# Attention's probabilities are scaled on ScalarE instead of VectorE, with one inverse per head and the four turns together

## The chip, the core and the metric

The kernel runs on one core of a Trainium2 chip. The metric is the device time of one launch in microseconds (us); three runs of the kernel before gave 2235.98, 2233.18 and 2235.42, so its median is 2235.42 us. The engines are named here as the profile names them: PE is TensorE (matmuls, with PEld for the weight loads that run beside them), DVE is VectorE, ACT is ScalarE, POOL is GpSimd and SP is SyncE, which only issues transfers. Each engine runs its own list of instructions strictly in order and waits on semaphores for the others.

## The reference

Two layers, each with an attention-like part and a feed-forward part, work on `x` of shape 4 x 512 x 512 (rows b, tokens, channels). Before each part the input is gated by a bidirectional recurrence (two scans over the tokens) over a side input. The change is in the second layer's attention: 16 heads in 4 groups, 128 channels a head, causal softmax:

```python
scores = jnp.einsum('bqgpd,bkgd->bgqpk', q, k) * (SCALE / LAYER_INDEX)
...
scores = jnp.where(causal[None, None, :, None, :], scores, -jnp.inf)
probs = jax.nn.softmax(scores, axis=-1).astype(x.dtype)
ctx = jnp.einsum('bgqpk,bkgd->bqgpd', probs, v).reshape(b, sq, HEADS * KVC)
return jnp.einsum('bse,eh->bsh', ctx, w_dense)
```

Everything is fp32. The softmax of a query row is exp(score - maximum) divided by the sum of these.

## The kernel before

The kernel runs four stages one after the other: the state-space layer, the routed experts (to about 1115 us), the attention (to about 1980 us), and the last feed-forward part. The change touches the attention alone.

The attention loops over 64 heads, numbered here h0 to h63 in the order group, row, head of the group: h0 to h3 are row 0 of group 0, h4 to h7 row 1 of group 0, and so on. For one head, `scores` (L1787) handles four strips of 128 queries. Strip `qi` needs keys up to (qi+1)*128, so the strips are 128x128, 128x256, 128x384 and 128x512. For each strip:

- PE multiplies into the PSUM tile `psc` (L1799). The tile comes from a pool of four that the keys `pk` and values `pv` of the next row also use, in turn. So the psc of the next head, strip by strip, needs the exp of the head before to have read its tile.
- DVE adds the causal mask (L1802) and takes the negated maximum `nmax` (L1804).
- `nudge()` issues a step of the gates for later parts (scans L259, L265 and elementwise work L276 to L333 on DVE; `f`, `eu`, `rec` on ACT), which are worked off beside the attention.
- ACT computes `pr` = exp(psc + nmax) and, in the same instruction, the sum `rsum` (L1809, which the profile shows as L128, the line of a helper; a short ACTIVATION_READ_ACCUMULATOR follows).
- DVE takes the inverse (L1810), multiplies `pr` by it (L1811), and turns it in 32x32 blocks into `turned` (L1815).

After the four strips POOL issues four transfers of `turned` to DRAM (L1823), and later `collect` (L1841) issues the one that brings the head back as `pT`, the transposed probabilities. `settle` runs `context` three heads later: PE multiplies `pctx` = v * pT (L1868), ACT copies it to `cx`, and when a row's four heads are there, `dense` multiplies them with w_dense into `pd` (L1887, four tiles of four products) and DVE adds it to the residual `xr` (L1895).

The last two heads (h62, h63; `turn` is true) keep their probabilities in SBUF, and PE turns them (L1854).

What sets the order: a scheduler builds each engine's list from the program; `with after(engine)` pins an instruction behind the one issued before it on that engine. From h13 to h61 (`even[0]` is true) the order on PE is pinned: psc, a query's products (pq, L1750), a key or value product, pctx, one of the four pd tiles. For h0 to h12 the scheduler places PE's work itself, and there all four pd tiles of a row stand together (13.7 us of PE). In the same stretch each new row b+1 of the residual must first be completed: ACT scales the expert results `rr` (L1537), DVE adds them (L1538), PE turns them into `pcb` (L1543), DVE adds that to `xr` (L1547); then ACT loads another activation table (L115), computes `th` of xr, DVE forms the gated input `h` (L406), ACT loads the exp table again, and PE starts the next row's `pq` (L1727), `pk` (L1699) and `pv` (L1710). `Tables.use` places a table load behind all exps, tanhs and the like issued before it; a plain multiply or copy on ACT is not among these. `pq` and `pcb` share a pool of two PSUM tiles.

```python
def ps_mm(name):
    return ps.tile([P, 512], F32, tag="mm", name=name, bufs=4)
```

Of the kernel before, what the change touches and what calls it, by code (L numbers as in the profile page):

```python
# [10 lines left out]
F32 = mybir.dt.float32  # L11
F32R = mybir.dt.float32r
I32 = mybir.dt.int32
AF = mybir.ActivationFunctionType
ALU = mybir.AluOpType
# [3 lines left out]
P = 128  # L19
B, T, C = 4, 512, 512  # L20
NC = C // P
NT = T // P
# [61 lines left out]
def block_kernel(ctx: ExitStack, tc: tile.TileContext, a: dict, out: bass.AP):  # L84
    nc = tc.nc

    @contextmanager
    def after(*engines):

        with ExitStack() as es:  # L90
            for e in engines:
                last = next(
                    (i for i in reversed(nc.cur_bb.bb.instructions) if i.engine == e.engine), None
                )
                if last is not None:
                    es.enter_context(tc.issue_after(last))
            yield
# [35 lines left out]
    act = Tables()  # L133
# [9 lines left out]
    def ps_mm(name):  # L143
        return ps.tile([P, 512], F32, tag="mm", name=name, bufs=4)
# [247 lines left out]
    def nudge():  # L392
        old = list(unsent)
        next(making, None)
        if old:
            send()
# [506 lines left out]
    with ExitStack() as ph:  # L903
# [5 lines left out]
        sm = ph.enter_context(tc.tile_pool(name="ssm", bufs=1, reuse_waits="tile"))  # L909
# [651 lines left out]
    with tc.tile_pool(name="moe_w2", bufs=1, reuse_waits="tile") as wm:  # L1561
# [33 lines left out]
        n = len(nc.cur_bb.bb.instructions)  # L1595
# [15 lines left out]
    with att as ph:  # L1611
        wdp = ph.enter_context(tc.tile_pool(name="att_wd", bufs=1, **right))
        sm = ph.enter_context(tc.tile_pool(name="att", bufs=2, **right))
# [70 lines left out]
        def in_turn():  # L1684
            return after(*[nc.tensor] * even[0])
# [101 lines left out]
        def scores(u, i, qT):  # L1787

            turn = u.last_row and i >= HPG - 2
            prs = []  # L1790
            if not turn:
                blocks = turned[next(numbers) % 2]
            for qi in range(NT):
                n = (qi + 1) * P
                if qi == 0:
                    collect(1)
                psc = ps_mm("psc")
                with in_turn():
                    nc.tensor.matmul(  # L1799
                        psc[:, :n], lhsT=qT[:, qi * P : n], rhs=u.kT[:, :n], start=True, stop=True  # L1800
                    )
                nc.vector.tensor_tensor(psc[:, qi * P : n], psc[:, qi * P : n], mask, ALU.add)  # L1802
                nmax = sm.tile([P, 1], F32, tag="nmax", name="nmax", bufs=4)
                nc.vector.tensor_reduce(nmax, psc[:, :n], AX.X, ALU.max, negate=True)  # L1804
                with after(nc.vector, nc.scalar):
                    nudge()
                pr = sm.tile([P, n], F32, tag=f"pr{qi}", name="pr")
                rsum = sm.tile([P, 1], F32, tag="rsum", name="rsum", bufs=4)
                act(pr, psc[:, :n], AF.Exp, bias=nmax, accum_out=rsum)  # L1809
                nc.vector.reciprocal(rsum, rsum)  # L1810
                nc.vector.tensor_scalar(pr, pr, rsum, None, ALU.mult)  # L1811
                if turn:
                    prs.append(pr)
                    continue
                nc.vector.transpose(  # L1815
                    blocks[:, :, 3 * qi : 4 * qi + 1, :].rearrange("p c k j -> p k c j"), pr
                )
            if turn:
                return prs
            d = turned_d.pop(0)  # L1820
            turned_d.append(d)
            for r in range(QUAD):
                nc.gpsimd.dma_start(  # L1823
                    out=d[:, :, r].rearrange("c i s -> i c s"),
                    in_=blocks[r * SQ : (r + 1) * SQ].rearrange("i c k j -> i c (k j)"),
                )
            away.append(d)
            return d
# [6 lines left out]
        def collect(rest=0):  # L1835

            while len(away) > rest:
                d = away.pop(0)
                back[id(d)] = pT = new_pT()
                with after(nc.gpsimd):  # L1840
                    nc.gpsimd.dma_start(  # L1841
                        out=pT.rearrange("p r k j -> p (r k j)"),
                        in_=d.rearrange("c i r s -> (c i) (r s)"),
                    )
# [128 lines left out]
        for n, (g, b, i) in enumerate(heads_):  # L1973
# [7 lines left out]
            if g == 2 and i == 0 and b < 3:  # L1981
                to, name = ((ffg_d, "gateT"), (ffu_d, "upT"), (ffd_d, "downT"))[b]
# [16 lines left out]
            if g == 0 and i == 2 and b + 1 < B:  # L1999
# [3 lines left out]
                act.use(act.LOG_EXP)  # L2003
                mix(b + 1, h)
            prs = scores(u, i, qT)
            if g == 0 and i == 1 and b + 1 < B:
                with after(nc.scalar):
# [23 lines left out]
    with ExitStack() as ph:  # L2031
        wf = ph.enter_context(tc.tile_pool(name="ff_w", bufs=1, reuse_waits="tile"))
        sm = ph.enter_context(tc.tile_pool(name="ff", bufs=2, **right))
# [201 lines left out]
```

## Time and profile before

| what | us |
|---|---|
| three runs | 2235.98, 2233.18, 2235.42; median 2235.42 |
| profiled execution, its time | 2229.05 |
| its span, first to last instruction | 2227.1 |
| outside the span (2229.05 - 2227.1) | 1.95 |
| PE busy | 2115.8 (95%) |
| DVE busy | 1584.9 (71%) |
| ACT busy | 952.4 (43%) |
| POOL busy | 500.2 (22%) |

The profiled execution is 6.4 us below the median of the three runs. Busy time is the sum of an engine's instructions; an engine that is idle has waited for something, and the profile names what came last. Two stretches of the attention differ:

| stretch, us from the span's start | PE busy | DVE busy | ACT busy | mean granted PE clock |
|---|---|---|---|---|
| 1115 to 1325 (h0 to h12) | 186.54 of 210 | 171.06 | 95.51 | 0.94 |
| 1325 to 1945 (the rest) | 615.54 of 620 | 468.37 | 218.26 | 0.99 |

### The profile page before, as it was taken

To read this page: it belongs to the slowest core of one execution; us is meant where nothing else is said; L and a number is where in the kernel's file an instruction comes from. 1 tells how busy PE (TensorE), PEld (TensorE's weight loads), DVE (VectorE), ACT (ScalarE), POOL (GpSimd) and SP (SyncE) were. 2 spreads that over 40 slices of the span, in tenths; PEclk is the share of its full clock that TensorE was granted. 3 is DMA by queue.
4 is the path that set the end of the run, shared out by engine and by line. 5 is a ranking of instruction groups with operands and counts; after the bars stand their busy time and mean duration, and the time that the engine had idled before them with its cause. 6 is when DMAs were issued, how large, how long until landed. Compare 5 with 4: busy or idle time off the path is not lost. (4 is left out here: it accounts for less than half of the span.)

```text
span 2227.1 us, 24718 instructions
## 1 busy us (share of the span) xinstructions
PE 2115.8 (95%) x7858; PEld 1283.1 (58%) x7858; DVE 1584.9 (71%) x3207; ACT 952.4 (43%) x1875; POOL 500.2 (22%) x668
## 2 busy tenths in 40 slices
PE   4979999999999999999988999999999999999998
PEld 2545565555665444444444446666666666568887
DVE  8698989999653566576479877788888766654332
ACT  4576676775732234333155433333333322333221
POOL 4023232422222111222233222222122222100000
PEclk9989999999999999999999999999999999999999
DMA  7542251442424458988577676767777565621100
GB/s 256 187 142 77 95 170 67 140 139 67 166 86 133 151 198 288 379 288 296 204 241 267 215 258 201 228 207 231 219 231 229 177 212 150 226 84 38 38 20 20
DMA packets 125512, 390.99 MB, mean 176 GB/s; under 512 B 15360, under 2 KB 36224, under 8 KB 111872
## 3 DMA queue, kind: packets, MB, share of 16 engines
q1 hardware_dynamic: 90560, 249.60, 32.6%
q0 software_dynamic: 32512, 135.55, 19.6%
q10 hardware_dynamic: 2304, 4.20, 0.5%
q8 instruction: 65, 1.06, 0.2%
q14 instruction: 71, 0.58, 0.1%
HBM read 363.07 MB, written 116.39 MB: 215 GB/s over the span
## 5 line engine op out<-in xcount | busy, mean ns | idle before, releaser
L128 ACT ACTIVATE pr<-psc,nmax 128x128 f32<-128x128 f32 (+3 forms) x256 | 134.1, 525 | 361.0 <-DVE nmax L1804 360.7
L1823 POOL DMA_DIRECT2D turned<-turned x248 | 135.7, 554 | 581.9 <-DVE turned L1815 501.5
L1887 PE MATMUL pd<-cx,wd 128*128 128x512 f32 x512 | 228.5, 593 | 0.0
L1799 PE MATMUL psc<-kT,qT 128*128 128x128 f32 (+3 forms) x512 | 158.0, 447 | 14.9 <-ACT pr L128 14.9
L1895 DVE TENSOR_TENSOR xr<-xr,pd 128x512 f32<-128x512 f32 x64 | 43.9, 685 | 175.5 <-PE pd L1887 175.4
L1868 PE MATMUL pctx<-pT,v 128*128 128x512 f32 (+3 forms) x512 | 151.9, 441 | 8.4 <-DMA pT<-turned 8.4
L1057 PE MATMUL pc<-h,wxb 128*128 128x512 f32 x320 | 145.5, 610 | 6.5 <-DVE h L406 4.0
L1887 PEld LDWEIGHTS pd<-cx,wd 128*128 128x128 f32 x512 | 93.8, 191 | 98.8 <-issue 97.4
L1868 PEld LDWEIGHTS pctx<-pT,v 128*128 128x128 f32 x512 | 97.1, 193 | 74.2 <-issue 51.1
L847 PE MATMUL po<-w,yT 128*128 128x512 f32 x296 | 134.1, 593 | 0.2 <-ACT yT L840 0.2
L814 PE MATMUL pg<-w,hT 128*128 128x512 f32 x296 | 134.2, 594 | 0.0
L825 PE MATMUL pn<-w,hT 128*128 128x512 f32 x296 | 133.3, 592 | 0.0
L1799 PEld LDWEIGHTS psc<-kT,qT 128*128 128x128 f32 x512 | 87.4, 193 | 69.7 <-issue 27.4
L1815 DVE STREAM_TRANSPOSE turned<-pr 128x128 f32<-128x128 f32 x248 | 120.4, 497 | 0.3
L1804 DVE TENSOR_REDUCE nmax<-psc 128x1 f32<-128x128 f32 (+3 forms) x256 | 120.1, 479 | 0.4
L1128 PE MATMUL pz<-wzt,h 128*128 128x512 f32 x256 | 116.1, 602 | 0.3 <-ACT st L1229 0.3
L1276 PE MATMUL po<-wot,yT 128*128 128x512 f32 x256 | 115.5, 605 | 0.0
L1057 PEld LDWEIGHTS pc<-h,wxb 128*128 128x128 f32 x320 | 60.9, 195 | 78.8 <-issue 72.8
L1811 DVE TENSOR_SCALAR pr<-pr,rsum 128x128 f32<-128x128 f32 (+3 forms) x256 | 103.8, 410 | 0.8
L1750 PE MATMUL pq<-ht,wq 128*128 128x256 f32 x384 | 98.5, 379 | 0.0
L1171 ACT ACTIVATE lm<-lm,cs 128x128 f32<-128x128 f32 x256 | 81.8, 390 | 22.5 <-DMA lm<-cs 22.5
L825 PEld LDWEIGHTS pn<-w,hT 128*128 128x128 f32 x296 | 54.8, 190 | 61.7 <-issue 61.7
(367 smaller groups left out, 4505.9 us busy)
## 6 DMA issues: line engine op xcount, KB each, us to landing
w<-in_w1x SPq DMA_DIRECT2D x76, 1024.0 KB
turned<-turned POOLq DMA_DIRECT2D x248, 208.0 KB, 4.0
pT<-turned POOLq DMA_DIRECT2D x62, 832.0 KB, 7.6
w<-in_w2x SPq DMA_DIRECT2D x38, 1024.0 KB
wb<-in_b1x SPq DMA_DIRECT2D x38, 512.0 KB
lm<-cs SPq DMA_DIRECT2D x32, 512.0 KB
kt<-in_fT SPq DMA_DIRECT2D x62, 256.0 KB
ek<-ek SPq DMA_DIRECT2D x62, 256.0 KB
```

The source lines that it names most:

```text
L128: nc.scalar.activation(*args, **kw)
L814: nc.tensor.matmul(pg, lhsT=hT[:, k, :], rhs=self.w1[s][0][:, k, :], start=(k == 0), stop=(k == NC - 1))
L825: nc.tensor.matmul(pn, lhsT=hT[:, k, :], rhs=self.w1[s][1][:, k, :], start=(k == 0), stop=(k == NC - 1))
L847: nc.tensor.matmul(po, lhsT=yT[:, j, :], rhs=self.w2[s][:, j, :], start=(j == 0), stop=(j == NI - 1))
L1057: nc.tensor.matmul(pc, lhsT=wxb[:, k, m * P : (m + 1) * P], rhs=h[:, k, :], start=(k == 0), stop=(k == NC - 1),)
L1128: nc.tensor.matmul(pz, lhsT=w.h[:, k, u.tok], rhs=wzt[:, k, hh * 512 : (hh + 1) * 512], start=(k == 0), stop=(k == NC - 1),)
L1799: nc.tensor.matmul(psc[:, :n], lhsT=qT[:, qi * P : n], rhs=u.kT[:, :n], start=True, stop=True)
L1804: nc.vector.tensor_reduce(nmax, psc[:, :n], AX.X, ALU.max, negate=True)
L1815: nc.vector.transpose(blocks[:, :, 3 * qi : 4 * qi + 1, :].rearrange("p c k j -> p k c j"), pr)
L1823: nc.gpsimd.dma_start(out=d[:, :, r].rearrange("c i s -> i c s"), in_=blocks[r * SQ : (r + 1) * SQ].rearrange("i c k j -> i c (k j)"),)
L1868: nc.tensor.matmul(pctx[:, kj * P :].rearrange("p (q r j) -> p q r j", r=QUAD, j=SQ), lhsT=u.v[:, kj, :], rhs=pT[:, :, 4 * kj : 10 + kj : ...
L1887: nc.tensor.matmul(po, lhsT=dense_w[u.g, m][:, i], rhs=u.ctxT[i], start=(i == 0), stop=(i == HPG - 1),)
```

## The change

Heads h0 to h61 are changed; h62 and h63 do what they did. The four sums of a head go into the columns of one 128x4 tile. After all four exps DVE takes one inverse of the 128x4 tile. ACT then multiplies each strip's `pr` by its column, in place, and DVE turns the strip. So per head four 128x1 inverses and four multiplies leave DVE, one 128x4 inverse comes to it, four multiplies come to ACT, and the four turns of a head, which stood each behind its own strip, stand behind the head's last exp. The transfers are the same and in the same order.

```diff
@@ -1788,6 +1788,7 @@
 
             turn = u.last_row and i >= HPG - 2
             prs = []
+            rsum = sm.tile([P, NT], F32, tag="rsum", name="rsum", bufs=2)
             if not turn:
                 blocks = turned[next(numbers) % 2]
             for qi in range(NT):
@@ -1805,18 +1806,20 @@
                 with after(nc.vector, nc.scalar):
                     nudge()
                 pr = sm.tile([P, n], F32, tag=f"pr{qi}", name="pr")
-                rsum = sm.tile([P, 1], F32, tag="rsum", name="rsum", bufs=4)
-                act(pr, psc[:, :n], AF.Exp, bias=nmax, accum_out=rsum)
-                nc.vector.reciprocal(rsum, rsum)
-                nc.vector.tensor_scalar(pr, pr, rsum, None, ALU.mult)
+                rs = rsum[:, qi : qi + 1]
+                act(pr, psc[:, :n], AF.Exp, bias=nmax, accum_out=rs)
+                prs.append(pr)
                 if turn:
-                    prs.append(pr)
-                    continue
+                    nc.vector.reciprocal(rs, rs)
+                    nc.vector.tensor_scalar(pr, pr, rs, None, ALU.mult)
+            if turn:
+                return prs
+            nc.vector.reciprocal(rsum, rsum)
+            for qi, pr in enumerate(prs):
+                nc.scalar.mul(pr, pr, rsum[:, qi : qi + 1])
                 nc.vector.transpose(
                     blocks[:, :, 3 * qi : 4 * qi + 1, :].rearrange("p c k j -> p k c j"), pr
                 )
-            if turn:
-                return prs
             d = turned_d.pop(0)
             turned_d.append(d)
             for r in range(QUAD):
```

## The prediction

> **What bounds the kernel now.** I read the page's engine rows first, then busy time by stretch, what PE's idle time waited for in each stretch, and single transitions on the timeline.
>
> ```profile
> PE 2115.8 (95%) x7858; PEld 1283.1 (58%) x7858; DVE 1584.9 (71%) x3207; ACT 952.4 (43%) x1875; POOL 500.2 (22%) x668
> ```
>
> PE is busy 95% of the span, and the change leaves PE's work as it is. So it can matter only where PE waits. Next the two stretches of the attention (columns: stretch, its length, busy time and count of PE, PEld, DVE, ACT and POOL, granted clock, DMA share, GB/s):
>
> ```profile
> 1115.00:1325.00 210.00, 186.54 (x611) 100.75 (x612) 171.06 (x373) 95.51 (x205) 69.87 (x99) 0.94 0.73 244
> 1325.00:1945.00 620.00, 615.54 (x2331) 398.14 (x2330) 468.37 (x1320) 218.26 (x560) 146.72 (x264) 0.99 0.68 210
> ```
>
> In the second stretch PE loses 4.5 us in 620, in the first 23.5 in 210. I call the first uneven, the second even. The uneven stretch's waits (what waits, total us, count, longest):
>
> ```profile
> PE psc L1799 <- ACT pr L128: 14.3, 11, 2.8
> PE pctx L1868 <- DMA pT<-turned: 5.5, 2, 5.2
> PE pcb L1543 <- DVE rr L1538: 2.0, 3, 0.7
> PE pq L1727 <- DVE xr L1547: 1.1, 3, 0.5
> ```
>
> The even stretch's:
>
> ```profile
> PE pctx L1868 <- DMA pT<-turned: 2.9, 1, 2.9
> PE ptp L1854 <- DVE pr L1811: 0.9, 1, 0.9
> PE psc L1799 <- ACT pr L128: 0.6, 1, 0.6
> ```
>
> So the even stretch has 4.4 us to give at most, and the change has to pay or cost among h0 to h12. There DVE is full wherever PE stalls (9.8 to 10.0 us of each 10 in 1140-1150, 1170-1180, 1190-1200, 1250-1260 and 1310-1320). The exps that psc waits for wait in turn for DVE's nmax.
>
> **The change, part by part.** The rows it touches, taken over the attention:
>
> ```profile
> L1810 DVE RECIPROCAL rsum<-rsum 128x1 f32<-128x1 f32 x256 | 36.6, 147 | 4.3 <-ACT pr L128 4.2
> L1811 DVE TENSOR_SCALAR pr<-pr,rsum 128x512 f32<-128x512 f32 x64 | 30.2, 472 | 0.3
> L1811 DVE TENSOR_SCALAR pr<-pr,rsum 128x384 f32<-128x384 f32 x64 | 27.6, 431 | 0.3
> L1811 DVE TENSOR_SCALAR pr<-pr,rsum 128x128 f32<-128x128 f32 x64 | 23.6, 369 | 0.1
> L1811 DVE TENSOR_SCALAR pr<-pr,rsum 128x256 f32<-128x256 f32 x64 | 23.5, 367 | 0.1
> L1537 ACT ACTIVATE rr<-rr,g 128x512 f32<-128x512 f32 x12 | 8.3, 720 | 2.6 <-DMA rr<-rows_o 2.5
> ```
>
> *DVE, per head:* four inverses (4 x 0.147 = 0.59) and four multiplies (0.369 + 0.367 + 0.431 + 0.472 = 1.64) go. One inverse of 128x4 comes; its nearest row is the 128x1 at 0.147, I take 0.15 (bounds 0.1 to 0.3, the latter a 128x128 operation's 0.28). Net -2.08 per head, -129 us over 62 heads. Some of the removed time is contention: one 128x128 multiply at 1266.93 runs on to 1271.5 beside POOL's work, where an undisturbed one takes 0.28.
>
> *ACT, per head:* four multiplies with a per-partition scale. The only such row is L1537, 720 ns for 512 columns; for the short ones the exps bound it (367, 469, 579 ns for 128, 256, 384). Sum 0.37 + 0.47 + 0.58 + 0.70 = 2.1 us. Successive instructions overlap by about 0.11 (two L1537 take 1.33), so a group stands for 1.75 us. Over 62 heads 130 us; in the even stretch ACT rises from 35% to about 52%, DVE falls from 76% to about 60%. Below 1.6 or above 2.3 us a head no row reaches.
>
> The Trainium skill ("ScalarE: Activation LUTs", "Rules for kernel authors") speaks against this: simple arithmetic such as multiplication belongs on VectorE, which is said to be faster per element. The rows here agree with the direction: 472 against 720 ns for 128x512. The same page ("What ACT_TABLE_LOAD costs") gives an activation with a per-partition pointer operand about 280 ns plus 0.833 ns a column; as an estimate that makes 2.19 us a head in place of 2.1, or 136 us over the kernel in place of 130. Neither decides, as ACT is half empty; what decides is what stands behind the four multiplies.
>
> *The even stretch.* The four multiplies wait for one inverse, which waits for the last exp; behind them on ACT stand kT or vT copies, the cx copy, and the next head's first exp. I followed the heads at 1506 and 1527. At 1527 the last exp could end at about 1533.8, as nmax no longer stands behind the four inverses and multiplies; multiplies to 1535.65; the kT copy waits for PE's pk at 1535.9, as before. The tightest reader is pd, which needs the fresh cx as its fourth product:
>
> ```profile
> 1537.95 3.60 PE L1887 MATMUL pd<-cx,wd 128*128 128x512 f32 x8
> 1538.21 0.60 ACT L1879 COPY cx<-pctx 128x512 f32<-128x512 f32 x1
> ```
>
> (first line PE, second ACT). It is read at about 1540.5, with the copy done at 1538.8; delayed by even a whole group of 1.75 us it would still be there. At 1506 cx comes about 2.5 us later (1516.7 for 1514.2), with 12 us before its use. The turns end 0.8 us earlier (1517.1 for 1517.9). So nothing in the even stretch costs PE anything; the pT wait of 2.9 us at 1725 shrinks by about 0.3, as the 128x512 turn ends that much earlier. **-0.3 us.**
>
> *The uneven stretch.* Between rows (in heads h1, h5, h9) the expert results are added on a chain that PE waits for: ACT scales rr, DVE adds (L1538), PE makes pcb, DVE adds xr, ACT th, DVE h, then PE's pq. Today rr follows the last exp (its accumulator is read at 1197.21) at once, and the table load lies behind it, under PE's and DVE's work:
>
> ```profile
> 1197.21 0.21 ACT L128 ACTIVATION_READ_ACCUMULATOR pr<-psc,nmax 128x1 f32 x1
> 1197.30 1.33 ACT L1537 ACTIVATE rr<-rr,g 128x512 f32<-128x512 f32 x2
> 1198.65 1.28 ACT L115 ACT_TABLE_LOAD   x1
> 1201.96 1.15 ACT L128 ACTIVATE th<-xr 128x512 f32<-128x512 f32 x2 [2.03 <-DVE xr L1547]
> ```
>
> In the built instruction lists of the changed kernel the order at all three transitions is: last exp, table load, the four multiplies, then rr. So rr comes 1.28 + 1.75 = **3.0 us** later, counted from the last exp. The last exp itself may come earlier, by what DVE is relieved of. PE's side of it today:
>
> ```profile
> 1197.47 2.08 PE L1799 MATMUL psc<-kT,qT 128*128 128x512 f32 x2 [1.28 <-ACT pr L128]
> 1199.49 1.71 PE L1543 MATMUL pcb<-ident,rr 128*128 128x128 f32 x8
> 1201.39 4.56 PE L1727 MATMUL pq<-h,wq 128*128 128x512 f32 x10 [0.19 <-DVE xr L1547]
> ```
>
> pcb already waits for rr at each transition (2.0 us in three waits above), so a later rr is a later PE.
>
> Followed instruction by instruction through DVE's, ACT's and PE's new orders with today's durations, it gives:
> - Row 0 to 1: the stalls of 1143 to 1152 (2.30 + 2.84 + 1.17) stay, since h0's four turns (1.68) now stand together between h1's nmax. PE is 3.0 late at pcb and 4.4 late at 1172 (three turns more between the adds to xr). Then psc's stalls there (1.02 + 1.19 + 1.31 = 3.5) vanish, because the multiplies of h3 no longer hold up its nmax. Left: **+0.9**.
> - Row 1 to 2: psc's third stall group (0.90 + 1.28) shrinks by 0.5, rr costs 3.0, and a wait of pk for 0.5 moves in with it: **+2.2** at 1210.
> - Row 2: DVE's order puts h7's softmax behind the adds from pd, so xr is 0.9 late for pq; h10's stall group grows from 1.95 (1.71 + 0.24) to 2.65: **+1.6**.
> - Row 2 to 3: rr costs 3.0; pcb's and pq's waits there (0.69 + 0.54) and the 4.57 us multiply at 1267 are gone, and only **+0.2** is left by pk.
>
> The wait of 5.2 us for pT at 1314 absorbs none of this: the transfer is issued behind h12's four turns, which come later with everything else. Sum at 1325: 0.9 + 2.2 + 1.6 + 0.2 = **4.9 us**.
>
> *The end.* h61's multiplies hold up h62's first exp by 1.5 us, which psc does not need yet: 0. After new stalls PE runs slower for a while (granted clock 0.81 in 1140-1150, where a 384-column psc pair took 1.65 us, not 0.91): **+0.5**.
>
> Sum 4.9 - 0.3 + 0.5 = +5.1: the profiled execution goes from 2229.05 to 2234.2. That execution is 6.4 under the median; moved onto the median, 2235.4 + 5.1 = **2240.5 us**.
>
> **The rivals.**
> - *No change that can be measured* (0.2%, 4.5 us, is what a measurement of this kernel can tell from none). DVE's relief returns as much as the transitions cost. For it: psc's waits are behind nmax, nmax behind the inverses and multiplies. Against it: the turns now come four in a row, 1.68 us, in front of nmax. About +1, 2236; it happens if half the 3 us at each transition is caught up (3 x 1.5 = 4.5 less).
> - *Faster: DVE bounds the uneven stretch.* Twelve and a half heads give back 12.5 x 2.08 = 26 us of DVE there. If all of psc's 14.3 and 0.6 and pT's 8.4 went, 23.3, it would be 2212. But the six us before the first transition stay, and rr's 9 us must be paid; with the rest of psc's stalls (8) and pT's (8.4) gone and 9 paid: -7.4, 2228. It decides where the last exp of h1, h5, h9 comes over 3.0 us earlier than now.
> - *Slower by more: nothing is caught up.* Three times 4.4 us = 13, with 0.5 of slow clock each: 2235.4 + 14.7 = 2250.
> - *The even stretch breaks:* if ACT's blocked list delays cx, kT or psc by 1 us in each of 12 rows, +12, 2247. Against it: the slack of 1.7 us that was read above, and PE's order is pinned.
>
> **How the numbers follow.** Slower at about 2240 has 0.38, slower by more (by either of the last two) 0.14; no change 0.33; faster 0.15. The likeliest one's own range is 2240 to 2246. The range for 8 in 10 leaves out the far half of either end: 2229 to 2250. Faster by over 0.2%: 0.15; within: 0.33; slower: 0.52.
>
> **What would show it.** DVE should fall to about 1456 us and ACT rise to about 1083. The even stretch should stay within 1 us of its length. At the three transitions the table load and four multiplies should stand between the last exp and rr, and PE's wait of pcb for rr should grow from 2.0 to some 8 us in all. psc's waits should fall from 14.3 to about 11. I am wrong if those transitions do not grow (then no change or faster), or if kT, cx or qT copies show up as what PE waits for in the even stretch.

## The result and the profile after

The changed kernel took 2245.63 us (median of six runs, 2243.79 to 2248.60), the kernel before 2235.28 beside it. The ratio is 1.0053, its 95% interval 1.0039 to 1.0068: slower by half a per cent, some 10 to 12 us, where 5 were forecast. The time lies in the forecast range and on its side. The size is the forecast's doubled, and it takes two steps of the sum to say why.

The busy time of the engines over the changed kernel's span of 2241.8 us, from the first part of its page:

```profile
PE 2121.6 (95%) x7858; PEld 1288.8 (57%) x7858; DVE 1506.7 (67%) x2773; ACT 1064.6 (47%) x2123; POOL 504.6 (23%) x668
```

The 248 multiplies are on ACT and 434 instructions have left DVE. PE has the same 7858 matmuls but 5.8 us more of busy time: it did the same work more slowly.

To find the place I laid fixed points of both traces side by side. The first `pk` of the attention starts at 1115.10 before and at 1119.58 after; these 4.5 us belong to work that both kernels have in common and are not the change's (over all traces of this study the point lies between 1113.88 and 1122.80). They are also why the two profiles lie 14.7 us apart (2229.05 and 2243.79), more than the medians do. From there to the first `pk` of the even stretch (1331.99 and 1349.23) the busy times are, before and after:

```profile
1115.10:1331.99 216.89, 193.53 (x636) 105.34 (x637) 175.36 (x388) 97.51 (x212) 70.99 (x101) 0.94 0.73 243
```

```profile
1119.58:1349.23 229.65, 198.67 (x636) 108.62 (x637) 148.18 (x287) 122.70 (x268) 71.20 (x100) 0.91 0.70 235
```

The stretch is 12.8 us longer. PE's busy time grew by 5.1 (193.53 to 198.67) at a lower granted clock (0.94 to 0.91), and its idle time by 7.6 (216.89 - 193.53 = 23.4; 229.65 - 198.67 = 31.0). DVE lost 27 us there, as intended, and ended up with more idle time. Behind it nothing is lost; in the changed kernel PE is busy without a break from 1344.48 to 1717.00:

```profile
1344.48:1717.00 372.52, 372.52 (x1436) 243.99 (x1435) 272.32 (x616) 192.31 (x467) 87.91 (x157) 1.00 0.71 220
```

and from 1349.23 to the end it is 2.5 us shorter than before (892.6 for 895.1). That is not less waiting but a faster clock: PE's busy time there is 881.9 for 884.9, and before has two spells of 3.4 us at a granted clock of 0.50 (from 1726.45 and 1934.66) that the changed kernel has not. What PE waited for in the first stretch after the change (total us, times, longest):

```profile
PE pcb L1543 <- DVE rr L1538: 11.8, 5, 3.7
PE psc L1800 <- ACT pr L128: 11.1, 11, 3.1
PE pctx L1871 <- DMA pT<-turned: 5.9, 1, 5.9
PE pk L1699 <- DVEq L1601: 2.4, 1, 2.4
PE pq L1727 <- DVE xr L1547: 1.5, 2, 0.9
PE pk L1699 <- ACT pr L128: 0.4, 1, 0.4
```

The `pk` wait for DVEq ends at the start of the stretch and lies ahead of it. Against the list of before: `pcb` rose from 2.0 to 11.8, `psc` fell from 14.3 to 11.1. Not all of `pcb`'s waits lie at the transitions: of the 2.0, 1.3 stand at 1128.08 and 1129.66, beside h0's first strips, and only 0.69 at a transition, the third; of the 11.8, 2.0 stand beside h0's strips and 2.64, 3.50 and 3.66 at the three transitions. So there the wait rose from 0.7 to 9.8. On ACT's timeline of the changed kernel the transition from the second to the third row shows the price of `pcb`:

```profile
1201.46 0.69 ACT L128 ACTIVATE pr<-psc,nmax 128x512 f32<-128x512 f32 x1
1202.03 0.21 ACT L128 ACTIVATION_READ_ACCUMULATOR pr<-psc,nmax 128x1 f32 x1
1202.26 1.28 ACT L115 ACT_TABLE_LOAD   x1
1203.56 1.92 ACT L1819 ACTIVATE pr<-pr,rsum 128x128 f32<-128x128 f32 x4
1205.38 1.32 ACT L1537 ACTIVATE rr<-rr,g 128x512 f32<-128x512 f32 x2
```

`rr` began 0.09 us after the last exp's accumulator read before (1197.21, 1197.30) and begins 3.35 us after it now (1202.03, 1205.38); at the other two transitions it is 3.32 and 3.33. The cause is a line that the diff does not touch: `combine(b + 1, (2, 3))`, which issues `rr`, stands behind `scores` under `with after(nc.scalar)`. That pins it behind whatever ScalarE was given last. Before that was the exp; now it is the fourth multiply, and the scheduler put the table load ahead of the multiplies too.

### The profile page after: what moved, and what is told of

It reads as the page before. It is cut to its first block, busy times and chain, and to the rows that moved or that the text cites. A ratio compares the mean times of both kernels' runs of the same rounds, so it can differ in the third digit from the quotient of the medians.

```text
span 2241.8 us, 24538 instructions
## 1 busy us (share of the span) xinstructions
PE 2121.6 (95%) x7858; PEld 1288.8 (57%) x7858; DVE 1506.7 (67%) x2773; ACT 1064.6 (47%) x2123; POOL 504.6 (23%) x668
## 4 chain that ended last, share of the span: by engine, by line
PE 43%; DVE 3%; DMA 2%; ACT 2%; issue 0%; SPq 0%; POOL 0%; DVEq 0%; POOLq 0%; ACTq 0%
PE pd L1890 10%; PE pq L1750 6%; PE pctx L1871 6%; PE psc L1800 4%; PE pv L1710 2%; PE pk L1699 2%; PE pfo L2068 2%; PE pfo L2067 2%; PE pfg L2067 2%; PE pfg L2068 2%; PE pfu L2067 2%; PE pfu L2068 2%; PE pq L1727 1%; DMA pT<-turned 1%; DVE turned L1820 1%; DMA rr<-rows_o 1%
## 5 line engine op out<-in xcount | busy, mean ns | idle before, releaser
L1800 PE MATMUL psc<-kT,qT 128*128 128x128 f32 (+3 forms) x512 | 155.1, 440 | 12.6 <-ACT pr L128 12.5
L1819 ACT ACTIVATE pr<-pr,rsum 128x128 f32<-128x128 f32 x248 | 118.9, 550 | 16.2 <-DVE rsum L1817 16.2
```

The source lines that it names most:

```text
L1800: nc.tensor.matmul(psc[:, :n], lhsT=qT[:, qi * P : n], rhs=u.kT[:, :n], start=True, stop=True)
```

## The experiments

Theory 1: the cost is made among h0 to h12, where `rr` stands behind multiplies and table load at three transitions, and PE, once it has waited, runs slower for a while. Rivals: ScalarE is too full in the even stretch; the single inverse and the four turns together are the cost, wherever the multiplies run; ScalarE's multiplies hold up exps anywhere in the first stretch.

Every row below is measured against the kernel before. The stretch is the one between these two `pk`; the waits are PE's in it, those of `psc` for the exp alone (in rr_act_only it waits 1.9 us more for a copy of kT).

| kernel | median us | ratio [95%] | stretch us | PE idle | PE busy | pcb | psc |
|---|---|---|---|---|---|---|---|
| before | 2235.28 | 1 | 216.89 | 23.4 | 193.5 | 2.0 | 14.3 |
| the change | 2245.63 | 1.0053 [1.0039, 1.0068] | 229.65 | 31.0 | 198.7 | 11.8 | 11.1 |
| late_only | 2233.05 | 0.9998 [0.9980, 1.0016] | 218.97 | 21.6 | 197.4 | 2.2 | 13.8 |
| early_only | 2246.15 | 1.0054 [1.0033, 1.0075] | 233.22 | 32.3 | 200.9 | 10.9 | 11.1 |
| rr_first | 2229.64 | 0.9974 [0.9955, 0.9992] | 215.55 | 22.2 | 193.3 | 1.8 | 12.5 |
| rr_first_2 | 2227.28 | 0.9984 [0.9967, 1.0001] | 213.49 | 22.1 | 191.4 | 1.8 | 12.6 |
| rr_act_only | 2230.43 | 0.9994 [0.9980, 1.0008] | 216.10 | 22.3 | 193.8 | 3.3 | 9.4 |
| trans_dve | 2232.79 | 1.0005 [0.9992, 1.0017] | 216.79 | 24.8 | 192.0 | 3.9 | 10.4 |
| dve_mul | 2238.41 | 1.0017 [0.9996, 1.0038] | 225.73 | 31.1 | 194.7 | 8.6 | 12.2 |
| dve_rr_first | 2233.24 | 0.9999 [0.9984, 1.0014] | 218.46 | 23.3 | 195.2 | 3.2 | 10.8 |
| per_strip | 2240.99 | 1.0041 [1.0026, 1.0056] | 220.46 | 25.0 | 195.4 | 7.9 | 11.4 |
| warm | 2238.60 | 1.0017 [1.0000, 1.0035] | 222.42 | 17.2 | 205.2, of it 15.9 idle products | 2.1 | 6.6 |
| double_even | 2254.30 | 1.0102 [1.0079, 1.0124] | 233.20 | 32.9 | 200.3 | 12.9 | 11.1 |

The before that the series of experiments ran beside had medians of 2232.81 to 2233.18, so ratios, not medians, are to be compared across rows. One profile a kernel stands behind the last five columns, and PE busy for the same instructions spreads: before and late_only do the same up to h12, and have 193.5 and 197.4.

### Where: late_only and early_only

With `n0` the number of the head, late_only keeps the form of before where `n0 < 13`, early_only where `n0 >= 13`:

```diff
+            old = n0 < 13
...
-                if turn:
+                if turn or old:
                     nc.vector.reciprocal(rs, rs)
                     nc.vector.tensor_scalar(pr, pr, rs, None, ALU.mult)
...
```

> The change for h13 to h61 alone; h0 to h12 keep the form of before. Theory 1 (the whole cost is made among h0 to h12, where rr waits behind the four multiplies): no change that can be measured, 0.998 to 1.002 of before, and PE's waits for psc, pcb and pT in the first stretch of the attention as before (14.3, 2.0, 5.5 us). Rival (ScalarE's blocked list also delays cx, kT or psc in the even stretch): a ratio of 1.003 or more, with new PE waits after h13.

> The change for h0 to h12 alone; h13 to h61 keep the form of before. Theory 1: all of the cost is here, a ratio of 1.004 to 1.007 as in the changed kernel (about +10 us), and PE's wait of pcb for rr among h1 to h12 about 9 us longer than the 2.0 of before. Rival (the even stretch carries the cost): 1.000 to 1.002.

Both came out as theory 1 had them: 0.9998 for 49 heads in the even stretch, 1.0054 for the 13 heads ahead of it, against 1.0053 for all. The rival of a full ScalarE in the even stretch is out: the multiplies of h13 to h61 cost nothing that can be measured.

### What: rr_first, trans_dve, rr_act_only

rr_first issues `rr` behind the last exp of h1, h5 and h9 (`between` is `combine(b + 1, (2, 3))` there, and empty for the other heads), and the head's inverse, multiplies and turns behind it:

```diff
-            nc.vector.reciprocal(rsum, rsum)
+            with ExitStack() as es:
+                if between:
+                    between()
+                    es.enter_context(after(nc.vector))
+                nc.vector.reciprocal(rsum, rsum)
...
```

> The whole change, but in h1, h5 and h9 the results rr are issued right behind the last exp, and the inverse, the four multiplies and the four turns of that head behind them. Theory 1 (the pin of rr behind the last instruction issued on ScalarE, now the fourth multiply, is the cause): pcb's waits for rr fall from about 12 us back to 2 to 5, PE's granted clock at the transitions recovers, and the time is 2231 to 2238. Rival (the grouped turns, or ScalarE's longer list among h0 to h12, cost on their own): the waits of pcb go, but the time stays above 2241, with other waits in their place.

The waits of `pcb` are gone, the time fell from 2245.6 to 2229.6, a little under the 2231 expected, and with the whole change in place it is under the kernel before. ACT's timeline of rr_first at the same transition:

```profile
1196.28 0.69 ACT L128 ACTIVATE pr<-psc,nmax 128x512 f32<-128x512 f32 x1
1196.85 0.21 ACT L128 ACTIVATION_READ_ACCUMULATOR pr<-psc,nmax 128x1 f32 x1
1196.94 1.34 ACT L1537 ACTIVATE rr<-rr,g 128x512 f32<-128x512 f32 x2
1198.30 1.28 ACT L115 ACT_TABLE_LOAD   x1
```

The load stands behind `rr` again, as it did before the change. PE's waits of rr_first in the stretch:

```profile
PE psc L1800 <- ACT pr L128: 12.5, 11, 3.1
PE pctx L1875 <- DMA pT<-turned: 3.5, 1, 3.5
PE pk L1699 <- DVEq L1601: 2.4, 1, 2.4
PE pq L1727 <- DVE h L406: 2.2, 2, 1.8
PE pq L1727 <- DVE xr L1547: 2.1, 2, 1.7
PE pcb L1543 <- DVE rr L1538: 1.8, 3, 0.8
```

New are 2.2 us for `h` and one more for `xr`, where the head's turns now stand; the transfer of pT is 2 us better. The repetition:

> The kernel of rr_first once more, beside the two others. It is expected at 0.996 to 0.999 of before, 2225 to 2231 us, as it measured 0.9974. If the ratio's interval reaches over 1.000 here, its gain over the kernel before is not settled.

It gave 0.9984, with the interval's end at 1.0001. By what was put on record, the gain over the kernel before is not settled; both series point to about 0.2%.

trans_dve gives h1, h5 and h9 the form of before, by the edit of late_only with `n0 in (1, 5, 9)`:

> The change in all heads but h1, h5 and h9, which keep the form of before (inverse, multiply and turn of each strip on VectorE). Theory 1 (three heads carry the cost): 2229 to 2236, pcb's waits among h1 to h12 2 to 5 us. Rival (the ten other heads of the first stretch cost too): 2239 or more.

2232.79, as theory 1 had it. Three heads of 62 carry the cost. The other ten of the first stretch cost nothing that can be measured.

rr_act_only is rr_first without the pin on VectorE (`es.enter_context(after(nc.vector))`):

> As rr_first, but only ScalarE's order is mended: rr stands right behind the last exp there, while inverse and turns of h1, h5 and h9 are left to the scheduler, which puts the four turns of h4 or h5 ahead of the add of rr between the second and the third row. If ScalarE's order alone decides: as rr_first, 2227 to 2233. If VectorE's order counts as well (turns that wait for the multiplies stand ahead of the add of rr): 2233 to 2241, with a wait of pcb of 2 us or more left at that one transition.

2230.43 lies in the first range, and rr_first_2, which ran beside it, lies within its interval (0.9984 in 0.9980 to 1.0008), so the time does not tell the two apart. The trace shows that VectorE's order does count: a `pcb` wait of 2.15 us is left at 1197, at the one transition where the turns stand ahead of the add of `rr`.

### How much is the grouping: dve_mul, dve_rr_first, per_strip

```diff
-                nc.scalar.mul(pr, pr, rsum[:, qi : qi + 1])
+                nc.vector.tensor_scalar(pr, pr, rsum[:, qi : qi + 1], None, ALU.mult)
```

> One inverse of four sums and the four turns together as in the change, but the four multiplies stay on VectorE. Theory 1: rr follows the last exp at once on ScalarE, and only the 0.3 to 0.6 us by which VectorE's multiplies stand ahead of the add of rr are left at each transition, so +0 to +3 us, 2234 to 2239. Rival (the single inverse and the turns together are the cost, wherever the multiplies run): +8 us or more, 2243 and above, with PE's psc and pT waits longer.

The time, 2238.41, lies in theory 1's range, but the way there was not what I wrote: `pcb` still waits 8.6 us. ScalarE's `rr` is prompt (at 1207.47, 0.10 us behind the last accumulator read at 1207.37), yet the four multiplies, which now come together behind the one inverse, stand ahead of the add of `rr` on DVE, and at the first transition the turns too. Of the 8.6 us, 5.3 lie at the three transitions (1.93, 1.17 and 2.19). PE's waits in dve_mul's stretch:

```profile
PE psc L1800 <- ACT pr L128: 12.2, 10, 4.0
PE pcb L1543 <- DVE rr L1538: 8.6, 5, 2.5
PE pctx L1871 <- DMA pT<-turned: 7.5, 2, 6.4
```

So the chain from `rr` to `pcb` can be blocked on either engine. That the grouping alone costs time is likely and not shown, as its ratio's interval reaches 0.9996. dve_rr_first is this edit on rr_first:

> The kernel of rr_first with the four multiplies on VectorE: rr is issued right behind the last exp in h1, h5 and h9, one inverse of four, four turns together. Theory 1 with a gain from the relief of VectorE: slower than rr_first by 2 to 6 us, 2232 to 2236, since the 26 us of multiplies and inverses are back on the engine that psc waits for. Rival (rr_first gains by the order alone, and where the multiplies run is worth nothing): the same as rr_first within 1.5 us.

0.9999: with `rr` first the grouping on DVE costs nothing that can be measured. It is 6 us above rr_first_2 and 3.6 above rr_first, as a gain from VectorE's relief would have it. But the intervals overlap, so that gain is likely and not shown.

per_strip keeps the multiplies on ScalarE, each with an inverse and a turn of its own:

```diff
+                nc.vector.reciprocal(rs, rs)
...
+                nc.scalar.mul(pr, pr, rs)
+                nc.vector.transpose(
+                    blocks[:, :, 3 * qi : 4 * qi + 1, :].rearrange("p c k j -> p k c j"), pr
+                )
...
-            nc.vector.reciprocal(rsum, rsum)
-            for qi, pr in enumerate(prs):
-                nc.scalar.mul(pr, pr, rsum[:, qi : qi + 1])
-                nc.vector.transpose(
...
```

> Four multiplies on ScalarE, but each strip has its own inverse, multiply and turn behind its exp, as before. Theory 1 (rr waits for what stands between the last exp and it on ScalarE): only one multiply of 0.7 us is left behind the last exp, so pcb's waits are 5 to 7 us and the time 2236 to 2241 in place of 2245.6. Rival (any multiply on ScalarE makes the exps wait for VectorE's inverses in between, strip by strip, which the grouping avoids): above 2246.

2240.99, at the upper end; `pcb` 7.9, a little above the 5 to 7, with 6.6 of it at the three transitions. The ratio's interval overlaps that of the change, so the gain over it is not shown by the time. On ACT's timeline of per_strip one sees what I left out, the table load, which stands ahead of the last multiply here too:

```profile
1197.35 0.19 ACT L128 ACTIVATION_READ_ACCUMULATOR pr<-psc,nmax 128x1 f32 x1
1197.56 1.28 ACT L115 ACT_TABLE_LOAD   x1
1198.86 0.72 ACT L1816 ACTIVATE pr<-pr,rsum 128x512 f32<-128x512 f32 x1
1199.49 1.32 ACT L1537 ACTIVATE rr<-rr,g 128x512 f32<-128x512 f32 x2
```

`rr` starts 2.1 us behind the accumulator read, not 0.7: of the changed kernel's 3.35, about 1.3 is the load and 1.8 the four multiplies. No run moves the load alone; its share is read off the timelines.

### The clock: warm

```diff
                 psc = ps_mm("psc")
+                if qi == NT - 1 and (u.g, i) == (0, 2) and u.b < B - 1:
+                    for _ in range(20):
+                        nc.tensor.matmul(
+                            psc[:, :P], lhsT=ident, rhs=ones, start=True, stop=True
+                        )
```

> The change, with twenty idle products of 128x128 (their result is overwritten) put on TensorE ahead of the last psc of h2, h6 and h10, where TensorE stands still for 2.6 to 3.7 us before pcb. Theory 1b (of the 12.8 us lost in the first stretch of the attention, 5.1 are a lower granted clock after these idle times): the same work of PE there goes back from 193.9 us towards 189, and the time from 2245.6 to 2239 to 2242, though PE has more to do. Rival (the clock does not follow the idle time, or the idle time is needed in any case): 2244 to 2248.

PE did 15.9 us more of work and the kernel became faster than the changed one: 2238.60, a little under the 2239 expected, and the intervals of the two ratios do not overlap. The products stand mostly where PE had waited: its idle time fell by 13.8 us (31.0 to 17.2), so they cost 2.1. The gain is in the other work: without them PE's busy time in the stretch is 205.2 - 15.9 = 189.3, against 198.7. PE's timeline of the changed kernel around the first transition (start, us, work, and in brackets the idle time before it):

```profile
1154.36 2.08 PE L1800 MATMUL psc<-kT,qT 128*128 128x512 f32 x2 [0.26 <-ACT pr L128]
1159.08 1.97 PE L1543 MATMUL pcb<-ident,rr 128*128 128x128 f32 x8 [2.64 <-DVE rr L1538]
1161.65 9.02 PE L1727 MATMUL pq<-h,wq 128*128 128x512 f32 x14 [0.61 <-DVE xr L1547]
```

the same `pq` in before:

```profile
1153.91 6.52 PE L1727 MATMUL pq<-h,wq 128*128 128x512 f32 x14 [0.36 <-DVE xr L1547]
```

and that of warm (40 records are 20 products; the last `psc` moved in between the two halves of `pcb`):

```profile
1157.09 6.31 PE L1801 MATMUL psc<-ones,ident 128*128 128x128 f32 x40 [0.25 <-ACT pr L128]
1163.24 0.60 PE L1543 MATMUL pcb<-ident,rr 128*128 128x128 f32 x4
1163.67 1.02 PE L1805 MATMUL psc<-kT,qT 128*128 128x512 f32 x2
1164.54 0.60 PE L1543 MATMUL pcb<-ident,rr 128*128 128x128 f32 x4
1164.97 5.32 PE L1727 MATMUL pq<-h,wq 128*128 128x512 f32 x12
```

A `psc` pair of 512 columns takes 2.08 us in the changed kernel and 1.02 in warm, the `pq` matmuls 0.64 and 0.44 each, and 0.47 in before. The granted clock of the changed kernel at the three transitions (columns as in the windows above, the clock behind POOL's count):

```profile
1150.14:1167.21 17.07, 11.24 (x19) 5.03 (x20) 14.69 (x29) 8.18 (x16) 4.43 (x7) 0.50 0.70 222
1204.75:1214.99 10.24, 7.20 (x15) 4.07 (x16) 6.64 (x12) 4.30 (x9) 2.19 (x4) 0.50 0.83 254
1273.02:1276.43 3.41, 3.41 (x10) 2.42 (x11) 3.38 (x7) 0.52 (x1) 1.77 (x4) 0.50 0.85 286
```

Over the stretch the clock was at half for 40.8 us in the changed kernel, 23.9 in before and 20.5 in warm. PE's work in this time was 30.0, 18.8 and, without the idle products, 14.6 us. Half of the differences, 5.6 us to before and 7.7 to warm, is what the slower clock should cost; measured are 5.1 and 9.4. So idle time at a transition can be paid twice, once as waiting and once as slower work behind it.

The second price does not go by the wait's length. `pcb` waited 2.64, 3.50 and 3.66 us at the three transitions, and half clock lasted 17.1, 10.2 and 3.4. Nor does it go by the idle time of the stretch: dve_mul's PE was idle as long as the changed kernel's (31.1 us) and had half clock for only 26.9 us and 194.7 us of busy time; late_only was idle for 21.6 and had 33.8 and 197.4.

The Trainium skill ("TensorE: Matmul & The Clock Gate", "What's actually happening") says that the clock is gated to half when TensorE has been idle for a window of about 3.4 us. The half is seen here, and the spells at half in the changed kernel last whole multiples of 3.4 us. That it takes one idle stretch of that length is not what these traces show: no gap ahead of the slow `pq` was as long as 3.4 (3.11, 0.26, 2.64 and 0.61 us, with 1.7 to 2.1 us of work between), and the clock was at half from 1150.14, behind the first 0.8 us of the first of them.

### The slack of the even stretch: double_even

```diff
                 nc.scalar.mul(pr, pr, rsum[:, qi : qi + 1])
+                if even[0]:
+                    nc.scalar.copy(pr, pr)
```

> The change, with a copy of each strip in place on ScalarE behind each of its multiplies, in h13 to h61 (about 1.9 us more per head, 93 us more of ScalarE). Theory 1 (the even stretch has ScalarE to spare, some 1.7 us before cx is late): 0 to +4 us on the changed kernel, 2245 to 2250, no new PE waits but single ones. Rival (it is full, and the change only just fits): +10 us or more, with PE waiting for cx, kT or psc.

2254.30, 8.7 above the changed kernel by medians and 11 by ratios (1.0102 and 1.0053 of before): about the rival's 10, and more than theory 1 allowed. ScalarE's busy time rose by 66.7 us (1064.6 to 1131.3), 1.36 a head, less than the 1.9 I expected. Of the profile, 3.6 us lie in the first stretch, which the edit does not touch (233.20 against 229.65, as in early_only), and 7.2 behind it (899.8 against 892.6). PE's waits of double_even behind that stretch:

```profile
PE pctx L1873 <- DMA pT<-turned: 7.8, 3, 3.1
PE psc L1800 <- ACT pr L128: 2.3, 1, 2.3
PE pd L1892 <- ACT cx L1884: 0.4, 1, 0.4
```

In the changed kernel they are 3.2, 1.4 and none, so they grew by 5.9 of the 7.2. So the even stretch has room for one set of multiplies and not for two, and what comes late first is the transfer of pT behind the turns, hardly the `cx` that I had called the tightest.

## Why the prediction was right in kind and short in size

- **The place and the mechanism held.** "The order at all three transitions is: last exp, table load, the four multiplies, then rr. So rr ... 3.0 us later": the trace has 3.3 (3.35 less 0.09), early_only has the whole cost, and rr_first takes it away. One reading on the way was wrong: "pcb already waits for rr at each transition (2.0 us in three waits above)". Of these three waits two lie beside h0's strips, and only the third transition had one (0.69).
- **The even stretch, "-0.3 us":** right as far as can be told. late_only measured 0.9998, in an interval of 0.18% (4 us) to either side, and the changed kernel's PE had no break up to 1717; 0.3 us itself is below what the runs resolve.
- **psc "from 14.3 to about 11":** 11.1. DVE's relief was worth what the working said, and it did make good the first transition: at the `psc` that starts at 1189.02 before and 1193.90 after, the loss stood at 0.4 us: 0.6 less idle time (0.9 more was forecast) and 1.0 of slower work.
- **"It gives: row 1 to 2 +2.2, row 2 +1.6, row 2 to 3 +0.2" was too low.** From that `psc` to the `pk` of the next row (1210.34 and 1220.61) the kernel lost 5.4 us, of them 3.7 idle time against the 2.2, and 7.0 more to the end of the stretch, of them 4.6 idle time against the 1.6 and 0.2; the rest is slower work. The working let psc's waits ahead of the second transition shrink by 0.5; they stayed at 0.90 and 1.28. At the third it let the later `rr` be absorbed but for 0.2; `pcb` waited 3.66 in place of 0.69. In all PE's idle time grew by 7.6, where 4.9 were forecast.
- **"After new stalls PE runs slower for a while: +0.5" was the term that failed most.** It measured 5.1 in the pair of profiles. With the other profiles, 200.0 on average in the three with `rr` late (the change, early_only, double_even) against 195.5 in before and late_only, it is 4.5. The clock shows where it comes from: 30.0 us of PE's work at half clock for 18.8. The row I quoted for it, a `psc` pair at 1.65 for 0.91 us, had about the right factor; I priced less than one such pair (0.5 for its 0.74) and not the 11.2, 7.2 and 3.4 us of work that ran at half clock at the three transitions.
- **Busy times, DVE "to about 1456 us" and ACT "to about 1083":** 1506.7 and 1064.6. I summed durations, and successive instructions overlap. DVE's busy time fell by 78 us and not 129. The durations of all its instructions sum to 1801.1 us before and 1680.4 after, 121 less; so 8 of the 129 never went, and 43 are overlap, 0.10 us for each of the 434 instructions. ScalarE gained 112 us over 62 heads, 1.81 a head, which is the distance in its timeline above (1203.56 to 1205.38). The path went by that distance (1.75) and was not touched by the mistake.

The changed kernel's own rows for the new instructions (form, count, busy us, mean ns):

```profile
L1817 DVE RECIPROCAL rsum<-rsum 128x4 f32<-128x4 f32 x62 | 10.8, 174 | 21.0 <-ACT pr L128 20.7
L1819 ACT ACTIVATE pr<-pr,rsum 128x128 f32<-128x128 f32 x62 | 24.8, 400 | 16.2 <-DVE rsum L1817 16.2
L1819 ACT ACTIVATE pr<-pr,rsum 128x256 f32<-128x256 f32 x62 | 30.6, 493 | 0.0
L1819 ACT ACTIVATE pr<-pr,rsum 128x384 f32<-128x384 f32 x62 | 37.2, 600 | 0.0
L1819 ACT ACTIVATE pr<-pr,rsum 128x512 f32<-128x512 f32 x62 | 43.8, 707 | 0.0
```

A head's four multiplies sum to 2.20 us and take 1.92, so each overlaps the next by 0.09. The Trainium skill's formula ("ScalarE: Activation LUTs", "What ACT_TABLE_LOAD costs") had given 2.19, my bound from the exps 2.1. The page's rule against multiplying on ScalarE, whose figure is for bf16, did not decide the case: the multiplies are slower there (707 for 472 ns at 128x512), but 49 heads of them cost nothing that can be measured.

What stays open: whether rr_first is faster than before at all, and how much of its 0.2% is VectorE's relief and how much the order; and what decides how long the clock stays at half behind a wait.

## What to carry to other kernels

When work moves to another engine, look for what was pinned behind the old last instruction of that engine: here a line that the diff left alone put the next row's inputs behind four multiplies and a table load, three times, and moving it back took away the whole +0.5%. Price a new wait of TensorE as the wait and, as a range, as slower work behind it: here from nothing (dve_mul's waits of 1.17 and 2.19 us) to 5.6 us (half of the 11.24 us of work in the spell of 17.1). And where an engine is half empty, its average says nothing about single places: three heads of 62 made the whole cost.

## What the runs showed of the hardware

- Around idle gaps of 0.3 to 3.1 us, close together, the granted clock was 0.50 for 17.1 us; 20 idle products of 128x128 ahead of the wait brought `pq` from 0.64 to 0.44 us a matmul.
- Waits of 2.64, 3.50 and 3.66 us stood beside spells at half clock of 17.1, 10.2 and 3.4 us.
- Taking 434 short instructions off DVE freed 0.10 us less for each than the summed durations fell by ((120.7 - 78.2) / 434); ScalarE's multiplies overlap by 0.09 us each ((2.20 - 1.92) / 3).
- One inverse of 128x4 takes 174 ns, four of 128x1 took 4 x 147.
